# Two graph-attention layers on one core: norm transposes moved from TensorE to VectorE blocks and a pass through DRAM

## The chip, the cores and the metric

The kernel runs on one core of one Trainium2 chip. The metric is the device time of one execution in microseconds, lower is better. The kernel before takes 2702.04 us, the median of three runs between 2700.38 and 2702.28. The engines are called PE (TensorE; PEld is its weight load), DVE (VectorE), ACT (ScalarE), POOL (GpSimd) and SP (SyncE, which here issues the DMAs).

## The reference

64 graphs of 256 nodes with 512 features pass through two layers, each with a norm without weights and a relu in front and a residual around it. All numbers are 32-bit floats.

```
h = relu(layernorm(x))                       # 64 x 256 x 512
hW = h @ W                                   # 512 -> 256
alpha = softmax(leaky_relu(hW a0 + (hW a1)^T) masked by adj)
x = x + concat(alpha @ hW, hW)
h = relu(layernorm(x))
q, k, v = h @ Wq.T + bq, h @ Wk.T + bk, h @ Wv.T + bv     # 8 heads of 64
x = x + concat(softmax(q k^T / 8 masked by adj) v) @ Wo.T + bo
```

Both norms feed matrix products that contract over the features. The normed rows have nodes on the partitions, and the products want features there, so every normed tile has to be transposed.

## The kernel before

**Groups and steps.** Two graphs make a group: 512 rows, as four tiles of 128 rows by 512 features (index `t` or `r`, 0 to 3). There are 32 groups, software-pipelined in `bounded`. While the main loop does the attention of group g, the generator `project(g+1)` makes q, k and v of the next group (21 pieces, named u in the order below), `outputs` multiplies a finished graph by Wo and adds it to x (7 pieces, o), and `first_layer(g+2)` (pieces named s) does the first norm, the whole first layer and the second norm of the group after that. One turn of the loop is a period of four steps. A step begins with `weigh` (products pr and total, then on DVE the reciprocal r and the product oT) and `scores` (products sc, on ACT the exponentials p, on DVE two multiplications of p by the mask, on POOL the sums ps). After that it runs the pieces in an order written out by hand:

```
steps = ("uosuoosuosoosuos", "uusususususu", "uosoosuosoosuos", "uusususususu")
```

I count the steps 0 to 3 and the s pieces of a period s1 to s20, five to a step.

**Products in seven.** `project` and `outputs` use seven products of half-size blocks in the place of eight. For that POOL makes sums of the operands (`operand_sums`, L374 to L379: tile sums for the projections, o_sums for the outputs), and results are added up in PSUM banks or by DVE. In `outputs` the piece o3 accumulates into the bank that o1's DVE addition (`add`, L626 to L628) must have read, o5 needs o3's, o6 needs o4's, o7 needs o5's. Five PSUM banks (tag turn) rotate among the short-lived products, three more are held.

**The norm.** `stats` (L338) takes mean and variance of a tile with two DVE instructions. `norm_T` (L343) makes the variances safe (ve, L347) and has POOL raise them to -1/2 (rstd, L349). Then for each tile `put` (L359) lets DVE make the normed tile xn (L354) one tile ahead, PE transposes it in four 128 by 128 blocks into one bank pt (through `transpose`, L116), and ACT takes the bank into hT with the relu (L365). In the first layer each hT tile is used at once by the products ph; in the second, four puts fill hT for `project`, after which POOL makes the sums and adds the output bias to x (L470, four instructions).

**What sets the order.** PE instructions keep the order of the program text (`in_order`, L107). On the other engines a list scheduler orders the instructions when the program is built: among those it takes for ready it prefers the earlier one of the text, so an instruction whose inputs are there early can go ahead of earlier text that still waits. `after` (L96) adds an order between two instructions without a semaphore; before the change only `weight_sums` uses it. Each engine then runs its queue strictly in that order. SP issues all DMAs: one load of 1 MB per group into tile x (L125) and one store of 512 KB per graph (L654).

**Start and end.** Group 0's first layer runs alone (`last_bias` and the weight sums of q are put in at its third GAP), then `project(0)` together with group 1's first layer, then the loop. `judge` (L224) computes bounds on the inputs; its pieces are put in where a norm has a gap, over many periods, and its 56 products use blocks of Wq and Wk that it loads again. At the end a branch on its result either stops or runs a general version, which doesn't run here.

Of the kernel before, what the change touches and what calls it, by code (L numbers as in the profile page):

```python
# [23 lines left out]
LARGEST_VALUE = 1e6  # L24

# [17 lines left out]
def bounded(  # L43
# [23 lines left out]
    nc = tc.nc  # L67
    B, N, D = x.shape
# [17 lines left out]
    psum = ctx.enter_context(tc.tile_pool(name="psum", bufs=1, space=bass.MemoryType.PSUM))  # L86

# [15 lines left out]


# [13 lines left out]
    xg = x.rearrange("(g b) (t p) d -> g p (b t) d", b=GB, p=P)  # L118
    og = out.rearrange("(g b) (t p) d -> g p (b t) d", b=GB, p=P)
# [3 lines left out]
    def load(g):  # L123
        xs[g] = big.tile([P, GT, D], F32, tag="x", name=f"x{g}", bufs=4)
        nc.sync.dma_start(xs[g], xg[g])  # L125

    load(0)


# [14 lines left out]
    for c in range(HP):  # L144
        for s in range(2):
            nc.vector.scalar_tensor_tensor(
                prod, w0_sb[:, c, 2:], 1.0, a_b[:, s, :], op0=ALU.mult, op1=ALU.mult,
                accum_out=w0_sb[:, c, s : s + 1],
            )
    edge = att.tile([P, NT, N], F32, tag="e", name="edge")  # L150
    nc.vector.tensor_scalar(edge, adj_i, 0.0, None, op0=ALU.not_equal)
# [6 lines left out]
    nc.vector.tensor_copy(maskT, pt)  # L158

    nc.vector.reduce_max(bad[:, 0, :], edge, axis=AX.X)  # L160
    nc.vector.tensor_scalar(bad[:, 0, :], bad[:, 0, :], 0.0, None, op0=ALU.is_equal)
    nc.vector.tensor_tensor(edge, edge, adj_i, op=ALU.not_equal)
    nc.vector.reduce_max(bad[:, 1, :], edge, axis=AX.X)

    load(1)
    load(2)
# [29 lines left out]
    rexp = const.tile([P, GT], F32, name="rexp")  # L196
    nc.gpsimd.memset(rexp, -0.5)
    ones = const.tile([P, P], F32, name="ones")
    nc.gpsimd.memset(ones, 1.0)

    def weight_sums(name):
        w = w_sb[name]
        first = nc.vector.tensor_sub(w[:, :, T3, :], w[:, :, W22, :], w[:, :, W12, :])
        after(first, latest[0])
        nc.vector.tensor_sub(w[:, :, T1, :], w[:, :, W12, :], w[:, :, W11, :])
        nc.vector.tensor_sub(w[:, :, T2, :], w[:, :, W22, :], w[:, :, T1, :])
        nc.vector.tensor_sub(w[:, :, T4, :], w[:, :, W21, :], w[:, :, T2, :])

    def last_bias():


        pb = mm("pb")
        for q in range(NQ):
            for half in range(2):
                b = small.tile([P, P], F32, tag="power", name=f"bv_{q}_{half}", bufs=1)
                nc.vector.tensor_scalar(b, ones, bv_col[:, half, q : q + 1], None, op0=ALU.mult)
                matmul(
                    pb, b, w_sb["o"][:, half, 2 * q : 2 * q + 2, :],
                    start=(q == 0 and half == 0), stop=(q == NQ - 1 and half == 1),
                )  # L220
        nc.vector.tensor_add(b_out, pb, b_out)


    def judge():  # L224
# [5 lines left out]
        nc.vector.memset(part, 0.0)  # L230
        junk = att.tile([P, D], F32, tag="junk", name="junk", bufs=1)

        def squares(col, *srcs):
            sums = small.tile([P, HP], F32, tag="sums", name=f"sums{col}", bufs=2)
            for i, src in enumerate(srcs):
                nc.scalar.activation(
                    junk[:, : src.free_size()], src, AF.Square, accum_out=sums[:, i : i + 1]
                )
            nc.vector.reduce_sum(part[:, col : col + 1], sums[:, : len(srcs)], axis=AX.X)

        for s in range(2):
            squares(s, w0_sb[:, :, s])
        squares(2, *[w0_sb[:, c, 2:] for c in range(HP)])
        wv = att.tile([P, HP, D // HP], F32, tag="block", name="wv_block", bufs=1)
        sums = small.tile([P, HP], F32, tag="sums", name="sums3", bufs=2)
        for c in range(HP):
            nc.sync.dma_start(
                wv, wvT[:, c * P : (c + 1) * P].rearrange("(c p) o -> p c o", p=P)
            )
            nc.scalar.activation(  # L250
                junk, wv.rearrange("p c o -> p (c o)"), AF.Square, accum_out=sums[:, c : c + 1]
            )
        nc.vector.reduce_sum(part[:, 3:4], sums, axis=AX.X)
        squares(4, bcol["q"])
        squares(5, bcol["k"])
        squares(6, bv_col.rearrange("p h q -> p (h q)"))
        nc.vector.reduce_max(part[:, 7:8], bad.rearrange("p a t -> p (a t)"), axis=AX.X)
        yield
        heads = const.tile([P, P], F32, name="heads")
        nc.vector.memset(heads, 0.0)  # L260
        for j in range(2):
            nc.vector.memset(heads[j * DH : (j + 1) * DH, j * DH : (j + 1) * DH], 1.0)
        rowsq = const.tile([P, 2, HP], F32, name="rowsq")
        for n, (name, src) in enumerate((("q", wqT), ("k", wkT))):
            for hp in range(HP):
                w = att.tile([P, HP, P], F32, tag="block", name=f"w{name}_block{hp}", bufs=1)
                nc.sync.dma_start(
                    w, src[:, hp * P : (hp + 1) * P].rearrange("(c p) o -> p c o", p=P)
                )
                yield  # L270
                gram = mm(f"gram_{name}{hp}")[:, :P]
                for c in range(HP):
                    matmul(
                        gram, w[:, c, :], w[:, c, :], start=(c == 0), stop=(c == HP - 1)
                    )
                a = small.tile([P, P], F32, tag="power", name=f"power_{name}{hp}_0", bufs=1)
                nc.vector.tensor_mul(a, gram, heads)
                yield
                for i in range(3):
                    square = mm(f"square_{name}{hp}_{i}")[:, :P]  # L280
                    matmul(square, a, a, start=True, stop=True)
                    if i < 2:
                        a = small.tile(
                            [P, P], F32, tag="power", name=f"power_{name}{hp}_{i + 1}", bufs=1
                        )
                        nc.vector.tensor_copy(a, square)
                    else:
                        nc.scalar.activation(
                            junk[:, :P], square, AF.Square, accum_out=rowsq[:, n, hp : hp + 1]
                        )  # L290
                    yield
        nc.vector.reduce_sum(part[:, 8:10], rowsq, axis=AX.X)
# [3 lines left out]
        nc.vector.tensor_scalar(norm, total, 1e-30, None, op0=ALU.add)  # L296
        power = const.tile([P, 10], F32, name="power")
        nc.gpsimd.memset(power, 0.5)
        nc.gpsimd.memset(power[:, 7:8], 1.0)
        nc.gpsimd.memset(power[:, 8:10], 1.0 / 32)  # L300
        nc.gpsimd.tensor_tensor(norm, norm, power, op=ALU.pow)
# [5 lines left out]
        nc.vector.tensor_add(test[:, 0:1], norm[:, 0:1], norm[:, 1:2])  # L307
        nc.vector.tensor_scalar(
            test[:, 0:1], test[:, 0:1], root / LARGEST_SCORE, None, op0=ALU.mult
        )  # L310
        nc.vector.tensor_scalar(side, norm[:, 8:10], root, None, op0=ALU.mult)
# [31 lines left out]
    def norm_T(src, mv, name):  # L343
# [15 lines left out]
        def put(t, dst):  # L359
            if t + 1 < GT:  # L360
                normed(t + 1)
# [34 lines left out]
    def first_layer(g):  # L396
# [11 lines left out]
        for t in range(GT + 1):  # L408
# [4 lines left out]
            if t == 0:  # L413
                continue
# [659 lines left out]
```

## Time and profile before

| | before |
|---|---|
| median of the timed runs | 2702.04 us |
| the profiled execution, its own time | 2699.08 us |
| span of the profile | 2697.3 us |
| mean granted TensorE clock | 0.993 |
| PE busy | 2620.4 us |
| DVE busy, instructions | 1669.7 us, 2558 |
| POOL busy | 1230.0 us |
| ACT busy | 835.9 us |
| DMA traffic, mean | 29 GB/s |
| xn, 128x512, DVE (L354) | 256 instructions, 893 ns mean, 523 to 1559 ns |
| statistics of a tile, DVE (L340) | 256 instructions, 680 ns mean |
| hT from pt, ACT (L365) | 256 instructions, 599 ns mean |

The profile is of one execution. Its span runs from the first to the last instruction; 1.8 us lie around it. In a row of the groups, the parts are line, engine, operation, output and inputs with their shapes and the count, then the busy time, the mean of one, and how long the engine stood idle before these instructions and what ended that. In the chain of waits each row is a start, a duration and what ran; it leads back from the last instruction to what released each one. In the windows view each stretch has busy time and number of instructions of PE, PEld, DVE, ACT and POOL, then the granted clock, the DMA share and GB/s. Busy PE time counts overlapping matmuls once, but the end of a matmul is modelled.

### The profile page before, as it was taken

The page shows a single profiled execution, that of the slowest core. Times are in us where ns is not written, and L with a number is a line of the kernel's source. Part 1 is how long each engine was busy: PE and PEld are TensorE (multiplying, and loading weights), DVE is VectorE, ACT ScalarE, POOL GpSimd, SP SyncE. Part 2 cuts the span into 40 slices and gives each one's busy share as a digit, 9 for nine tenths or more (in the row PEclk, how much of TensorE's full clock was granted, in tenths as well). Part 3 has the DMA queues.
Part 4 walks back from the last instruction along what each step waited for, and adds up shares of the span by engine and source line. Part 5 has one row for each costly group of instructions (what it writes and reads, how often), then busy time and mean ns, then how long its engine had stood idle before and what let it go on. Part 6 is the DMA issues. An engine that isn't in the chain of part 4 may idle for free.

```text
span 2697.3 us, 41512 instructions
## 1 busy us (share of the span) xinstructions
PE 2620.4 (97%) x17150; PEld 2118.8 (79%) x17150; DVE 1669.7 (62%) x2558; ACT 835.9 (31%) x1771; POOL 1230.0 (46%) x1004
## 2 busy tenths in 40 slices
PE   5999999999999999999999999999999999999997
PEld 3888888878888887887788888788878878878874
DVE  5666566666557665566665576665576656666544
ACT  2333232333332333323333323333333333233321
POOL 2353355443445443545434454435455335445343
PEclk8999999999999999999999999999999999999998
DMA  5000101000001010000000000000000000000000
GB/s 164 1 12 32 36 24 36 13 32 32 28 32 36 9 36 32 24 32 9 32 32 24 32 32 9 32 32 24 32 32 9 32 32 24 32 17 23 17 16 25
DMA packets 45890, 78.49 MB, mean 29 GB/s; under 512 B 3712, under 2 KB 10624, under 8 KB 45696
## 3 DMA queue, kind: packets, MB, share of 16 engines
q1 hardware_dynamic: 45696, 75.77, 8.1%
q8 instruction: 137, 2.24, 0.3%
q14 instruction: 57, 0.47, 0.1%
HBM read 42.21 MB, written 33.55 MB: 28 GB/s over the span
## 4 chain that ended last, share of the span: by engine, by line
PE 89%; DVE 8%; POOL 1%; issue 1%; DMA 0%; ACT 0%; DVEq 0%
PE pq L113 15%; PE pv L113 14%; PE py L113 13%; PE pk L113 13%; PE pr L113 9%; PE ph L113 8%; PE sc L113 7%; PE po L113 4%; PE pt L116 4%; DVE p L573 3%; DVE r L604 2%; PE total L113 2%; DVE k L544 1%; DVE oT L605 1%; PE pn L116 1%
## 5 line engine op out<-in xcount | busy, mean ns | idle before, releaser
L573 DVE TENSOR_TENSOR p<-p,maskT 128x1024 f32<-128x1024 f32 x256 | 398.6, 1588 | 0.6 <-ACT p L572 0.5
L572 ACT ACTIVATE p<-sc 128x512 f32<-128x512 f32 x512 | 264.4, 602 | 380.9 <-PE sc L113 380.9
L574 POOL TENSOR_TENSOR ps<-p 128x512 f32<-128x512 f32 x256 | 366.2, 1447 | 0.0
L628 DVE TENSOR_TENSOR x<-py,x 128x256 f32<-128x256 f32 x448 | 187.6, 419 | 272.8 <-PE py L113 266.9
L604 DVE RECIPROCAL r<-total 128x256 f32<-128x256 f32 x128 | 224.5, 1754 | 194.6 <-PE total L113 194.6
L113 PE MATMUL py<-wo_sb,o_sums 128*128 128x256 f32 x1024 | 266.5, 384 | 26.4 <-DVE x L628 21.6
L420 POOL TENSOR_TENSOR x<-H,x 128x256 f32<-128x256 f32 x128 | 87.7, 685 | 443.0 <-ACT H L419 441.9
L113 PE MATMUL pr<-p,v 128*32 128x256 f32 x4096 | 251.8, 385 | 5.8 <-DVE p L573 5.8
L113 PE MATMUL sc<-q,k 64*128 64x256 f32 x2048 | 255.7, 389 | 0.0
L113 PE MATMUL pq<-sums,wq_sb 128*128 128x256 f32 x1024 | 246.7, 384 | 4.2 <-POOL sums L377 3.7
L113 PE MATMUL ph<-w_sb,hT 128*128 128x258 f32 x1024 | 246.1, 383 | 0.0
L113 PE MATMUL pk<-sums,wk_sb 128*128 128x256 f32 x1024 | 244.8, 382 | 0.0
L113 PE MATMUL pv<-wv_sb,sums 128*128 128x256 f32 x1024 | 242.0, 379 | 0.1
L113 PEld LDWEIGHTS sc<-q,k 64*128 64x128 f32 x2048 | 187.2, 186 | 69.7 <-issue 52.6
L113 PEld LDWEIGHTS py<-wo_sb,o_sums 128*128 128x128 f32 x1024 | 191.2, 192 | 62.9 <-POOL o_sums L377 37.6
L365 ACT ACTIVATE hT<-pt 128x512 f32<-128x512 f32 x256 | 153.1, 599 | 266.0 <-PE pt L116 265.7
L354 DVE TENSOR_SCALAR xn<-x,mv,rstd 128x512 f32<-128x512 f32 x256 | 225.8, 893 | 9.5 <-PE pt L116 4.9
L376 POOL TENSOR_TENSOR o_sums<-oT 128x256 f32<-128x256 f32 x64 | 106.2, 1660 | 262.6 <-DVE oT L605 262.6
L113 PEld LDWEIGHTS pq<-sums,wq_sb 128*128 128x128 f32 x1024 | 190.1, 191 | 39.1 <-issue 9.9
L113 PEld LDWEIGHTS ph<-w_sb,hT 128*128 128x128 f32 x1024 | 195.7, 192 | 28.6
L113 PEld LDWEIGHTS pk<-sums,wk_sb 128*128 128x128 f32 x1024 | 189.3, 190 | 33.9 <-issue 9.9
L113 PEld LDWEIGHTS pr<-p,v 128*32 128x32 f32 x4096 | 121.1, 110 | 112.2 <-issue 39.7
(145 smaller groups left out, 4054.4 us busy)
## 6 DMA issues: line engine op xcount, KB each, us to landing
x<-in_x_dram SPq DMA_DIRECT2D x32, 1024.0 KB, 5.5
out_dram<-x SPq DMA_DIRECT2D x64, 512.0 KB, 2.8
wq_sb<-in_L_gnn_Wq_dram SPq DMA_DIRECT2D x2, 512.0 KB, 11.7
wk_sb<-in_L_gnn_Wk_dram SPq DMA_DIRECT2D x2, 512.0 KB, 12.4
wv_sb<-in_L_gnn_Wv_dram SPq DMA_DIRECT2D x2, 512.0 KB, 11.4
wo_sb<-in_L_gnn_Wo_dram SPq DMA_DIRECT2D x8, 128.0 KB, 3.3
wv_block<-in_L_gnn_Wv_dram SPq DMA_DIRECT2D x4, 256.0 KB, 3.0
wq_block<-in_L_gnn_Wq_dram SPq DMA_DIRECT2D x4, 256.0 KB, 2.9
```

The source lines that it names most:

```text
L113: in_order(nc.tensor.matmul(*args, **kwargs))
L116: in_order(nc.tensor.transpose(*args))
L354: latest[0] = nc.vector.tensor_scalar(xn[t], src[:, t, :], mv[:, t, 0:1], rstd[:, t : t + 1], op0=ALU.subtract, op1=ALU.mult,).ins.name
L365: nc.scalar.activation(dst, pt, AF.Relu)
L376: nc.gpsimd.tensor_add(sums[:, 0], a21, a22)
L420: nc.gpsimd.tensor_add(xt[:, t, F1:], H[:, t, 2 : F1 + 2], xt[:, t, F1:])
L544: nc.vector.tensor_add(part(1, 1), first, p7)
L572: nc.scalar.activation(pair[:, j], sc[j], AF.Exp, scale=scale)
L573: nc.vector.tensor_mul(pair, pair, maskT[:, None, :, :].to_broadcast([P, 2, NT, N]))
L574: nc.gpsimd.tensor_add(ps[:, 2 * i : 2 * i + 2, :], pair[:, :, 0, :], pair[:, :, 1, :])
L604: nc.vector.reciprocal(r, total)
L628: nc.vector.tensor_add(to, out, to)
```

## The change

From group 1 on, the four transposes of a tile leave PE. `turn` (two tiles, one graph, at a time) has DVE transpose each xn inside 32 by 32 blocks (one instruction for a tile), SP stores the result to a scratch tensor in DRAM (passed, 512 KB), and four more DMAs of 128 KB read it back with the blocks moved to their place (moved). ACT applies the relu from moved, in SBUF, into hT. Group 0 still uses PE. Each GAP between `turn` and `put` is a piece s at which the generator issues nothing more.

A wrapper remembers the latest instruction of each engine in the order of the text, and `not_sooner` puts an instruction behind it: statistics, xn and the DVE transposes on DVE, the relu on ACT, the first of the operand sums on POOL. The bias additions to x leave `first_layer` and are issued in step 1. `judge` runs at the start, takes its blocks from the weights in SBUF, and does four products per bank. x is loaded by graph, in seven buffers of 512 KB; hT0 becomes one buffer for a graph; the three kept buffers become two of one tag. `last_bias` uses POOL for its four columns, each in its own place. The order string of the steps is the same.

```diff
+    def not_sooner(engine, operation, *args, **kwargs):
+        last = engine.last
+        after(getattr(engine, operation)(*args, **kwargs), last)
...
-    def load(g):
-        xs[g] = big.tile([P, GT, D], F32, tag="x", name=f"x{g}", bufs=4)
-        nc.sync.dma_start(xs[g], xg[g])
+    def load(g, b):
+        xs[g, b] = big.tile([P, NT, D], F32, tag="x", name=f"x{g}_{b}", bufs=7)
+        nc.sync.dma_start(xs[g, b], xg[g, b])
...
+        if vector.last:
+            not_sooner(vector, "bn_stats", st, src[t])
...
+        def norm(b):
+            tiles = slice(b * NT, (b + 1) * NT)
+            ve = small.tile([P, NT], F32, tag="ve", name=f"ve{name}_{b}")
+            vector.tensor_scalar(ve, mv[:, tiles, 1], EPS, None, op0=ALU.add)
+            rstd = small.tile([P, NT], F32, tag="rstd", name=f"rstd{name}_{b}")
+            gpsimd.tensor_tensor(rstd, ve, rexp, op=ALU.pow)
+            for t in range(NT):
+                r = b * NT + t
+                xn[r] = att.tile([P, D], F32, tag="xn", name=f"xn{name}_{r}", bufs=2)
+                not_sooner(
+                    vector, "tensor_scalar", xn[r], src[r], mv[:, r, 0:1], rstd[:, t : t + 1],
+                    op0=ALU.subtract, op1=ALU.mult,
+                )
+        def turn(b):
...
+            J = P // S
+            xt = att.tile([P, J, HP, NT, S], F32, tag="xt", name=f"xt{name}_{b}")
+            moved = att.tile([P, J, HP, NT, S], F32, tag="moved", name=f"moved{name}_{b}")
+            passed = dram.tile([P, J, HP * NT * S], F32, tag="passed", name=f"passed{name}_{b}")
+            for t in tiles:
+                not_sooner(
+                    vector, "transpose",
+                    xt[:, :, :, t % NT, :], xn[t].rearrange("p (c j a) -> p j c a", j=J, a=S),
+                )
+                turned[t] = moved[:, :, :, t % NT, :].rearrange("p i c n -> p c i n")
+            nc.sync.dma_start(passed, xt.rearrange("p j c t n -> p j (c t n)"))
+            for j in range(J):
+                nc.sync.dma_start(
+                    moved[j * S : (j + 1) * S].rearrange("a i c t n -> a i (c t n)"),
+                    passed.rearrange("(i a) j e -> j a i e", a=S)[j],
+                )
+        def put(b, dst):
+            for t in range(NT):
...
+                    not_sooner(scalar, "activation", to, turned[b * NT + t], AF.Relu)
...
     def operand_sums(quads, sums):
         a11, a12, a21, a22 = quads
-        nc.gpsimd.tensor_add(sums[:, 0], a21, a22)
+        not_sooner(gpsimd, "tensor_add", sums[:, 0], a21, a22)
...
     def first_layer(g):
...
+        norm(0)
         yield GAP
...
+        turn(0)
+        norm(1)
+        yield GAP
+        turn(1)
+        yield GAP
+        yield GAP
+        put(0, hT[0])
+        yield GAP
+        for r in range(GT):
...
+            if r == NT - 1:
+                put(1, hT[1])
             yield
...
             stats(mv, xt, r, f"1_{g}")
+            if r == 2:
+                norm(0)
+            elif r == 3:
+                turn(0)
+            yield
...
+        norm(1)
         yield GAP
+        turn(1)
+        yield GAP
+        put(0, hT[:, :, :N])
+        yield GAP
+        put(1, hT[:, :, N:])
...
-        for t in range(GT):
-            nc.gpsimd.tensor_add(xt[:, t, :], xt[:, t, :], b_out)
-        yield
+        yield
+
+    def residual(g):
+        for b in range(GB):
+            for t in range(NT):
+                xt = xs[g, b][:, t, :]
+                gpsimd.tensor_add(xt, xt, b_out)
...
+    verdict = judge()
+    for piece, _ in enumerate(first_layer(0)):
+        if piece == 9:
+            next(verdict)
+        if piece == 14:
             last_bias()
+            next(verdict)
+        if piece == 16:
             weight_sums("q")
+    residual(0)
...
-            if step == 1 and g + 3 < NG:
-                load(g + 3)
+            if step == 1 and g + 1 < NG:
+                residual(g + 1)
+            if step % 2 and g + 3 < NG:
+                load(g + 3, b)
```

With it the s pieces of a period hold: s1 the four statistics and `norm(0)` of the first layer; s2 `turn(0)` and `norm(1)`; s3 `turn(1)`; s4 nothing; s5 `put(0)`; s6 to s9 ph, with `put(1)` at s7; s10 pn and e; s11 nothing; s12 to s15 po with its statistics, `norm(0)` of the second layer at s14 and `turn(0)` at s15; s16 `norm(1)`; s17 `turn(1)`; s18 `put(0)`; s19 `put(1)` and the operand sums.

## The prediction

> **What bounds the kernel now.** I read the page first: shares, then the chain that ended last.
>
> ```profile
> PE 2620.4 (97%) x17150; PEld 2118.8 (79%) x17150; DVE 1669.7 (62%) x2558; ACT 835.9 (31%) x1771; POOL 1230.0 (46%) x1004
> ...
> PE 89%; DVE 8%; POOL 1%; issue 1%; DMA 0%; ACT 0%; DVEq 0%
> ```
>
> PE holds nearly all of the span; no other engine has two thirds of it. A share hides the stages, so the windows view comes next, for the four steps of one late period (rows in order: step 0, 1, 2, 3).
>
> ```profile
> 1994.66:2015.14 20.48, 20.48 (x141) 16.82 (x144) 10.86 (x14) 6.74 (x14) 12.10 (x10) 1.00 0.00 1
> 2015.14:2037.76 22.62, 22.62 (x149) 18.54 (x152) 7.69 (x9) 8.08 (x19) 7.09 (x6) 1.00 0.19 70
> 2037.76:2058.12 20.36, 19.35 (x129) 15.41 (x132) 15.92 (x29) 4.96 (x11) 6.56 (x5) 1.00 0.00 1
> 2058.12:2076.42 18.30, 18.30 (x133) 14.70 (x136) 17.21 (x27) 6.02 (x11) 12.68 (x10) 1.00 0.08 30
> ```
>
> The period is 81.76 us. PE is idle for 1.0 us of it, in step 2, and the granted clock is full. DVE (the third busy time) is unequal: 17.2 us of 18.3 in step 3, 10.9 of 20.5 in step 0. Whatever leaves PE shortens the period, until DVE is late for it.
>
> The chain in order of time gives PE's pitch, and DVE's timeline its queue, from the start of a step 0 at 2076.42.
>
> ```profile
> 2076.42 1.86 PE pr L113 x32
> ...
> 2086.89 0.44 PE pt L116 x4
> 2087.32 1.73 PE pq L113 x8
> ```
>
> ```profile
> 2078.78 1.76 DVE L604 RECIPROCAL r<-total 128x256 f32<-128x256 f32 x1 [3.16 <-PE total L113]
> 2080.58 0.69 DVE L605 TENSOR_TENSOR oT<-pr,r 128x512 f32<-128x512 f32 x1
> 2081.18 3.23 DVE L573 TENSOR_TENSOR p<-p,maskT 128x1024 f32<-128x1024 f32 x2
> 2084.34 0.41 DVE L628 TENSOR_TENSOR x<-py,x 128x256 f32<-128x256 f32 x1
> ```
>
> A tile's four transposes hold PE for 0.44 us (the 156.2 us of busy time are 152 ns for each, with overlap; the pitch is 109 ns). DVE starts r when total ends and reaches o1's addition 7.92 us into the step.
>
> **Removed from PE.** 31 groups by 8 tiles by 0.435 us: **-107.9 us** (busy time would say -151; the chain decides). That none of it is saved is the other end.
>
> **judge.** Its 112 instructions at 0.108 us (the chain has 0.22 for two of its squares; 12.1 us) leave later steps for the first 100 us. There PE is busy 48.4 of the first 80 us, so up to all 12 can hide: **-6**, between -12 and 0. Its loads vanish from an idle queue: nothing.
>
> **Start.** The chain has 5.74 us of bias additions on POOL (53.57 to 59.31) ahead of the sums that the third product waits for; they now come after. The four rounds of last_bias (45.40 to 52.80) no longer alternate with DVE. Against that, group 1 turns on DVE beside `project(0)`, whose pieces are 1.73 us apart, so s2 to s6 is some 8 us and the round trip below is 8 to 9. **-6**, between -15 and +5. Sum so far: 2697.3 - 107.9 - 6 - 6 = **2577.4**, if nothing else is late.
>
> **Added to DVE.** 248 transposes of 128x512. The trace has none. Nearest rows:
>
> ```profile
> L354 DVE TENSOR_SCALAR xn<-x,mv,rstd 128x512 f32<-128x512 f32 x256 | 225.8, 893 | 9.5 <-PE pt L116 4.9 <-POOL rstd L349 3.6 <-issue 0.2
> L604 DVE RECIPROCAL r<-total 128x256 f32<-128x256 f32 x128 | 224.5, 1754 | 194.6 <-PE total L113 194.6
> L340 DVE BATCH_NORM_STATS2 st<-x 128x6 f32<-128x512 f32 x256 | 169.1, 680 | 15.8 <-DMA x<-in_x_dram 4.9
> ```
>
> I take 0.69 (L340's 0.68; additions of 128x512 take 0.69): 171 us, DVE 1841 in all. Ends: 0.52 (the fastest xn) and 1.75 (the reciprocal); no less than nothing, since it is an instruction more.
>
> The Trainium skill speaks against this edit. "VectorE: DVE Perf Modes", section "The three transpose paths", gives 311 ns for 128x128 bf16 on VectorE, within 32 by 32 blocks only, and its "Rules for kernel authors" give a 128x128 transpose to TensorE when PSUM will do. By that rule the tile's 0.44 us stay on PE and the time stays at 2697; by the busy shares it pays to move them. An estimate from the page's figure is four times 311 ns, 1.24 us a tile, 0.55 above my value.
>
> **Moved on DVE.** Statistics, xn and transposes no longer fill DVE's holes, but stand behind earlier text. Step 3 is relieved; step 0, 17.4 us of PE without its three pts (1.3) and its ph (1.74), now holds DVE work of 9.1 (10.86 less two xn) + 4 x 0.85 statistics + 4 x 0.9 xn + 4 x 0.69 + 0.3 = 19.2 us. By hand, in us from the step's start: o1's addition ends at 8.3; four statistics (0.75 apart) at 11.3; ve 11.4; while POOL makes rstd (its ps end at 11.9, 1.0 more), the additions of u2, o2, o3 end at 12.8; two xn at 14.7; two transposes at 16.0; ve; o4's addition at 16.5. PE, with its pieces at 1.73 (u) and 0.865 (o), has o5 done at 13.9 and then stands at o6, whose bank waits for o4's addition: **2.6 us**. Should rstd be later, o4's addition goes first and the stall is nothing, but the norm is later by as much. Today such waits are small:
>
> ```profile
> PE py L113 <- DVE x L628: 21.6, 27, 1.0
> ```
>
> Step 1 takes over the ph (23.9 us; DVE about 10 and the spill) and step 3 has slack. In step 2 DVE gets 15.9 + 1.8 + 1.3 less the hoisted 1.3, some 17.7 of 20.4 us: the 1.0 stays. Loop turns 0 to 29 do this: 30 x 2.6 = **+78**, between 0 (DVE's holes suffice) and 200 (below).
>
> **The round trip.** SP waits for both transposes, stores 512 KB and waits for that to land before it issues four loads of 128 KB.
>
> ```profile
> out_dram<-x SPq DMA_DIRECT2D x64, 512.0 KB, 2.8
> wq_block<-in_L_gnn_Wq_dram SPq DMA_DIRECT2D x4, 256.0 KB, 2.9
> ```
>
> With 0.37 us per issue: 0.4 + 2.8 + 4 x 0.4 + 2.9 = 7.7 us (5.9 if the loads land at once, 9 if each of them is like wo_sb's 3.3 under load). Behind the waits SP queues the out store and the x loads; x is read a period later, so nobody waits. Some 130 MB more over 2650 us are 49 GB/s on top of 29; the load phase reaches 400.
>
> First layer: transposes at 16.0, moved at 23.7, relu 25; ph is due at 17.4 + 2.6 + 7.7 = 27.7. Hidden. Second layer: `turn(1)` in step 3 runs at about 14.5 (r to p end at 8.3 there, v's addition, rstd 1.0 to 2.4, two xn, transposes), moved at 22.1, which is 5.6 into the next step 0; relu 6.8; two sums (1.28 each) 9.4; u3 needs them at 10.5. Hidden by 1.1 us. Relu from SBUF: ACT's nearest row is 630 ns (wv_block) against 599 from PSUM, 8 us on an engine at 31%: nothing.
>
> "DMA: Bandwidth & Descriptors", section "Two DMAs through the same engine are not ordered", says that a transfer must wait for the first one's completion count; the trace agrees (load L125 after the store into its buffer waited 74.5 us in 28 times), and the 2.8 us can't be overlapped.
>
> **Bias additions to x.** Same four instructions of POOL in step 1 (7.1 of 22.6 us busy) in place of step 3 (12.7 of 18.3): nothing. Other edits (two kept buffers, one hT0, seven x buffers): their next use is two pieces or more away, nothing; a kept buffer that isn't free would cost a piece, 1.7 us.
>
> **Forecast.** 2577.4 + 78 = 2655.4 of span. The profiled execution lies 1.8 above its span, and the median 3.0 above that: **2660**.
>
> **Rivals.**
> - *Hidden altogether* (DVE in the holes, stall 0): 2577.4 + 4.7 = 2582. For it: DVE 62%, and a list scheduler fills rstd's wait. Against: 19.2 us into 17.4.
> - *The round trip takes the wait over* (slower). `put(1)` stands in ACT's queue ahead of step 0's exponentials. They are ready 3.45 us into the step (ACT's timeline), moved 5.6: with two relus they start 3.4 late, and masks, o1's addition and o3's product with them. Price 30 x (2.6 + 3.4) = 180: 2577.4 + 180 + 4.7 = **2762**. It decides from 4.0 us a period on (119.9 / 30), so from some 1.4 us of lateness. For it: such waits of ACT exist today:
>
> ```profile
> ACT hT L365 <- PE pt L116: 265.7, 156, 17.3
> ```
>
> Against: if the scheduler knows the latency, it puts the exponentials first.
> - *A transpose costs like the reciprocal*, 1.75: o4's addition 2.1 later and the second pair as much, 2.6 + 4.2 = 6.8 a period: 2577.4 + 30 x 6.8 + 4.7 = 2786.
> - *It doesn't do what it says*, the round trip being waited for at every relu of the first layer too (7.7 a half group): above 2800, or the transposes staying: 2690.
>
> **How the numbers follow.** Forecast 0.36 (stalls of 1.3 to 3.7: its own range 2620 to 2693), hidden 0.26, near no change (stalls near 4.0) 0.06, round trip 0.23, dear transposes 0.05, the last 0.04. A measurement of this kernel tells some 0.2% from no change (5 us). Faster: 0.36 + 0.26 = 0.62; same 0.06; slower 0.23 + 0.05 + 0.04 = 0.32. The range 2580 to 2750 leaves out the upper half of the round trip and the dear transposes.
>
> **What would show it.** Right: pt only 32 instructions; DVE transposes near 0.69; a period near 80.3 with step 0 near 20 and PE's largest wait "py <- DVE x", some 2.6 us a period; step 3 near 16.5; POOL's sums ending some 9 us into step 0. Wrong: PE without waits and a period of 78 (hidden); or ACT standing at hT for DMA, and then PE waiting for p, o_sums or kept (round trip); or a transpose above 1 us.

## The result and the profile after

The changed kernel takes **3034.62 us** (median of 4 runs, 3032.70 to 3035.32), the kernel before 2701.21 us (2699.42 to 2702.28): a ratio of **1.1234**, 95% interval 1.1214 to 1.1253. The forecast was 2660 us, in a range of 2580 to 2750. It is wrong in its sign and by 375 us.

The shares first, then the engines of the chain that ended last, from the page of the kernel after.

```profile
PE 2665.9 (88%) x16158; PEld 2112.8 (70%) x16158; DVE 1743.9 (58%) x2847; ACT 821.5 (27%) x1759; POOL 1200.1 (40%) x1072
...
PE 68%; POOL 16%; DVE 13%; issue 2%; ACT 1%; DMA 0%; SPq 0%; ACTq 0%; DVEq 0%; POOLq 0%
```

PE has 992 instructions fewer (248 tiles of four transposes), and yet more busy time than before, 2665.9 against 2620.4. POOL, with 1% of the chain before, holds 16% of it. POOL's busy share says nothing of it (it fell from 46% to 40%); the chain says who is waited for.

The windows view of one late period, in the order step 1, 2, 3, 0 (columns: the stretch, its length, the busy time of PE, PEld, DVE, ACT and POOL with the number of their rows, PE's granted clock, DMA share, GB/s).

```profile
1615.18:1639.10 23.92, 23.92 (x152) 19.67 (x156) 8.10 (x9) 9.45 (x23) 7.71 (x7) 1.00 0.34 96
1639.10:1663.30 24.20, 21.08 (x129) 16.60 (x132) 16.07 (x32) 4.95 (x11) 8.54 (x8) 0.93 0.00 1
1663.30:1680.38 17.08, 16.77 (x116) 13.13 (x120) 13.87 (x18) 4.87 (x9) 9.09 (x8) 1.00 0.51 172
1680.38:1707.33 26.95, 20.48 (x120) 15.90 (x124) 15.81 (x29) 6.07 (x13) 11.90 (x11) 0.81 0.12 42
```

The period is 92.15 us, 10.39 longer than before: step 1 +1.30, step 2 +3.84, step 3 -1.22, step 0 +6.47. Thirty times that is 312 of the 333 us; another 16 lie ahead of the loop (the first pr starts at 143.31 instead of 126.97). Step 1 is what the forecast had (23.9), and step 3 is 0.6 us over its 16.5. The loss sits in the two steps that hold `outputs`, and in both the clock column falls below 1.00.

Who makes PE wait, from the waits view of PE (us in total, times, longest):

```profile
PE py L135 <- POOL o_sums L35: 301.1, 63, 6.5
```

Twice a period PE stands at o3, the first product that needs an operand sum of the outputs. Before, PE waited 4.2 us in all for o_sums, and its largest wait was 21.6. POOL's timeline in step 0, which starts at 1680.38, shows why the sum is late.

```profile
1686.44 1.26 POOL L35 TENSOR_TENSOR ps<-p 128x512 f32<-128x512 f32 x1 [9.93 <-DVE p L35]
1687.66 3.47 POOL L35 TENSOR_TENSOR sums<-hT 128x512 f32<-128x512 f32 x2
1691.10 1.26 POOL L35 TENSOR_TENSOR sums<-sums,hT 128x512 f32<-128x512 f32 x1
1692.43 1.27 POOL L35 TENSOR_TENSOR sums<-hT,sums 128x512 f32<-128x512 f32 x1
1693.66 1.26 POOL L35 TENSOR_TENSOR ps<-p 128x512 f32<-128x512 f32 x1
1694.88 0.72 POOL L35 TENSOR_TENSOR o_sums<-oT 128x256 f32<-128x256 f32 x1
1695.67 0.72 POOL L35 TENSOR_TENSOR o_sums<-o_sums,oT 128x256 f32<-128x256 f32 x1
```

The operand sums come last. In the text `scores`, which holds ps, stands ahead of `outputs`, and `not_sooner` on the first operand sum puts it behind whatever POOL's instruction was last in the text: both ps, which wait for the exponentials and for DVE's masks. Before, the scheduler had taken the three o_sums ahead of the ps, 5.3 to 9.4 us into the step. POOL's rows in the kernel before, in a step 0 that starts at 1994.66:

```profile
1999.92 1.71 POOL L376 TENSOR_TENSOR o_sums<-oT 128x256 f32<-128x256 f32 x1
2001.70 1.59 POOL L377 TENSOR_TENSOR o_sums<-o_sums,oT 128x256 f32<-128x256 f32 x1
2003.37 0.73 POOL L379 TENSOR_TENSOR o_sums<-oT,o_sums 128x256 f32<-128x256 f32 x1
2004.06 2.50 POOL L574 TENSOR_TENSOR ps<-p 128x512 f32<-128x512 f32 x2
```

Now oT, which the o_sums need, is there at 1685.2 and they start at 1694.88, behind both ps and the four projection sums. PE's rows around the gap:

```profile
1688.95 1.03 PE L135 MATMUL py<-wo_sb,oT 128*128 128x256 f32 x4
1696.45 2.07 PE L135 MATMUL py<-wo_sb,o_sums 128*128 128x256 f32 x4 [6.47 <-POOL o_sums L35]
1698.32 3.62 PE L135 MATMUL pq<-sums,wq_sb 128*128 128x256 f32 x8
```

Behind the gap a piece of project takes 3.4 us up to the next row instead of 1.73, and a piece of outputs 1.9 instead of 0.865: the granted clock is 0.81 over this step. In step 2 the same happens at a smaller scale: both ps end at 1648.5, o_sums at 1650.0, PE waits 3.12 us, clock 0.93. Against their usual pitch the rows behind the two gaps are stretched by 2.9 and 1.8 us.

### The profile page after: what moved, and what is told of

Same layout as the page of the kernel before. It is cut to its first block, busy times and chain, and to the rows that moved or that the text cites. A ratio compares the mean times of both kernels' runs of the same rounds, so it can differ in the third digit from the quotient of the medians.

```text
span 3032.3 us, 40906 instructions
## 1 busy us (share of the span) xinstructions
PE 2665.9 (88%) x16158; PEld 2112.8 (70%) x16158; DVE 1743.9 (58%) x2847; ACT 821.5 (27%) x1759; POOL 1200.1 (40%) x1072
## 4 chain that ended last, share of the span: by engine, by line
PE 68%; POOL 16%; DVE 13%; issue 2%; ACT 1%; DMA 0%; SPq 0%; ACTq 0%; DVEq 0%; POOLq 0%
PE pk L135 11%; PE py L135 11%; PE pq L135 11%; PE pv L135 9%; PE pr L135 7%; PE ph L135 7%; POOL ps L35 6%; POOL sums L35 6%; PE po L135 4%; DVE r L35 4%; DVE p L35 4%; PE sc L135 3%; POOL o_sums L35 3%; PE total L135 2%; DVE oT L35 1%
## 5 line engine op out<-in xcount | busy, mean ns | idle before, releaser
L35 POOL TENSOR_TENSOR ps<-p 128x512 f32<-128x512 f32 x256 | 396.9, 1561 | 600.9 <-DVE p L35 600.9
L135 PE MATMUL py<-wo_sb,o_sums 128*128 128x256 f32 x1024 | 307.1, 434 | 301.1 <-POOL o_sums L35 301.1
L35 DVE TENSOR_TENSOR p<-p,maskT 128x1024 f32<-128x1024 f32 x256 | 374.4, 1485 | 21.7 <-ACT p L35 21.6
L135 PE MATMUL pq<-sums,wq_sb 128*128 128x256 f32 x1024 | 299.6, 445 | 9.3 <-POOL sums L35 8.8
L35 POOL TENSOR_TENSOR o_sums<-oT 128x256 f32<-128x256 f32 x128 | 145.8, 1139 | 385.2 <-DVE oT L35 383.5
L35 POOL TENSOR_TENSOR rstd<-ve,rexp 128x2 f32<-128x2 f32 x128 | 90.8, 710 | 501.1 <-DVE ve L35 484.6
L135 PEld LDWEIGHTS pq<-sums,wq_sb 128*128 128x128 f32 x1024 | 228.7, 226 | 61.5 <-ACT p L35 9.9
L35 DVE TENSOR_SCALAR xn<-x,mv,rstd 128x512 f32<-128x512 f32 x256 | 178.1, 708 | 162.5 <-POOL rstd L35 162.4
L35 DVE TENSOR_TENSOR k<-pk,kept_k 128x512 f32<-128x512 f32 x96 | 66.1, 688 | 317.2 <-PE pk L135 317.0
L35 ACT ACTIVATE kept_q<-pq,bq_sb 128x256 f32<-128x256 f32 x192 | 81.1, 479 | 564.4 <-PE pq L135 564.4
L135 PEld LDWEIGHTS pv<-wv_sb,sums 128*128 128x128 f32 x1024 | 194.5, 190 | 28.5 <-DVE v L35 2.1
## 6 DMA issues: line engine op xcount, KB each, us to landing
wq_sb<-in_L_gnn_Wq_dram SPq DMA_DIRECT2D x2, 512.0 KB, 10.9
```

The lines of the kernel that those rows point to most:

```text
L35: instruction = getattr(self.engine, operation)(*args, **kwargs)
L135: in_order(nc.tensor.matmul(*args, **kwargs))
```

## The experiments

Theory *order*: most of the loss is the order of the operand sums on POOL. Rival *trip*: it is the passes through DRAM, which make hT and the projection's sums late. Rival *VectorE*: transposes and their orders make DVE late, as the forecast's own term of 78 us has it. A fourth share, *rest*, is judge, the moved bias additions and the buffers.

**The operand sums freed**: one line of the changed kernel.

```diff
-        not_sooner(gpsimd, "tensor_add", sums[:, 0], a21, a22)
+        gpsimd.tensor_add(sums[:, 0], a21, a22)
```

> The changed kernel with one line put back: the first of the operand sums on POOL is no longer ordered behind the last POOL instruction of the text. Theory order (o_sums stand behind both ps, which wait for the masks; PE waits for them at o3 in steps 0 and 2): the wait py <- o_sums (301 us) all but goes, the period falls from 92.15 to about 83.6 us, the time to about 2780; what stays is a wait of pq <- sums of some 4 us at u3, because the second norm arrives late from DRAM. Theory round trip (the late arrival alone fills POOL's place for the o_sums): the sums still come ahead of o_sums, the wait moves little, time above 2950. Theory of the forecast (DVE is late for o4's addition): no change, since DVE's order is the same.

Measured: 2831.53 us, ratio 1.0487 (1.0469 to 1.0504), period 85.76: 203 us and 6.4 us a period under the changed kernel. PE's waits now:

```profile
PE pq L135 <- POOL sums L35: 119.6, 32, 6.9
PE py L135 <- DVE x L35: 47.0, 88, 1.8
...
PE py L135 <- POOL o_sums L35: 4.2, 2, 2.1
```

The wait at o_sums is gone, and another takes its place once a period: in step 0, u3 waits 3.67 us for the projection's sums. Of the 47.0 us at x, 27.1 lie in step 2, where the kernel before has its 21.6; the other 19.9 lie in step 0, at o6 and behind it. There the wait is 1.81 us (with 0.46 and 0.16 behind it) in only two of 30 periods, whose clock column reads 1.00; in the others the clock is lower behind the gap at u3 (0.93 or 0.86), PE comes later to o6, and less of this wait or none is left. Step 0 lasts 24.5 us either way. So order is the largest share and not the whole.

**The order alone, put on the kernel before**: the first operand sum goes behind the last ps, whose name `pool_last` holds; nothing else.

```diff
-        nc.gpsimd.tensor_add(sums[:, 0], a21, a22)
+        first = nc.gpsimd.tensor_add(sums[:, 0], a21, a22)
+        if pool_last[0]:
+            after(first, pool_last[0])
```

> The kernel before with one order added: the first operand sum behind the last ps of the text. All transposes stay on PE. Theory order: PE gets the wait py <- o_sums in steps 0 and 2, 1 to 3 us in each and something on top for a lower granted clock, so 100 to 180 us more, 2800 to 2880. Theory round trip or DVE: within 10 us of 2702.

Measured: 2877.41 us, ratio 1.0655 (1.0637 to 1.0673). PE's wait for o_sums is 151.2 us in 63 times (mostly 1.75 us in a step 0, 3.12 in a step 2). The period isn't steady: it lies between 85.9 and 90.9 us (median 87.6), with a step 2 of 22.5, 24.2 or 25.4 us; the last section shows why. One dependency that computes nothing costs 178 us in a kernel without any pass through DRAM. By an estimate some 125 of them are waits (151.2 less the 4.2 for o_sums and the 21.6 for x that they replace) and some 53 the clock (0.975 granted over the span of 2880.1 us, against 0.993 of 2697.3). With the trip beside it the same order costs 203, because the late projection sums stand between ps and o_sums in POOL's queue (the rows above).

**All tiles turned by PE**, all orders kept.

```diff
-        by_pe = g == 0
+        by_pe = True
```

> The changed kernel with every transpose on PE (group 0's way for all groups): no DVE transposes, no pass through DRAM, all the orders and moves kept. Theory order: still far above before, 2800 to 2880, with py <- o_sums as the first wait of PE. Theory round trip: near 2700 or below, since judge and the start alone save some 12 us. Theory DVE: between, since the transposes' 5.4 us a period leave DVE.

Measured: 2997.68 us, ratio 1.1102 (1.1083 to 1.1120), period 91.3 (median). A miss for all theories: no tile passes through DRAM and the time is still 11% over. The wait for o_sums is 159.0 us in 63 times as in the run above, and PE now waits for xn (38.6 us in 31 times, of which 26.7 in step 0, 0.92 a time), because the ordered xn come late and the transposes stand in PE's own order. Another 22.2 us are a wait of sc for ACT's exponentials, which the run with all tiles on PE and everything free takes up. Where the orders stay, moving the transposes back buys 37 us.

**Second norm on PE, operand sums freed**: the first norm still passes through DRAM.

```diff
-        norm, turn, put = norm_T(xt, mv, f"1_{g}", by_pe)
+        norm, turn, put = norm_T(xt, mv, f"1_{g}", True)
```

> The changed kernel with the operand sums free, and the second norm transposed by PE (the first by DVE and DRAM). The sums of the projections can start as early as before. Theory order plus late arrival: no large wait is left, the period is 81.8 less four transposes of a tile (1.7 us), near 80, time 2620 to 2650. If the DRAM pass of the first norm or DVE's longer queue costs PE, ph <- hT or py <- x shows it and the time is above 2680.

Measured: 2727.20 us, ratio 1.0100 (1.0083 to 1.0117), period 82.38, first pr at 127.56. 104 us under the run with both norms through DRAM: the second norm's pass is a loss, though it takes 124 tiles off PE. The first norm's isn't seen as a wait for DRAM. What is left is the forecast's own stall, "py <- DVE x", 81.6 us in 114 times: 52.9 in step 0, where the forecast has it, and 26.3 in step 2, where the kernel before has it too. My expectation was 77 us or more too low: it left out that stall and the rest's 40 us, measured further on.

**All of the norms' instructions free, both norms through DRAM.** From here on, "free" also takes `not_sooner` off the statistics, xn, the VectorE transposes and the relus.

```diff
-                not_sooner(
-                    vector, "tensor_scalar", xn[r], src[r], mv[:, r, 0:1], rstd[:, t : t + 1],
-                    op0=ALU.subtract, op1=ALU.mult,
-                )
+                vector.tensor_scalar(
+                    xn[r], src[r], mv[:, r, 0:1], rstd[:, t : t + 1],
+                    op0=ALU.subtract, op1=ALU.mult,
+                )
```

> The run with the operand sums freed, and also the orders taken off the statistics, xn, the VectorE transposes and the relus; both norms still pass through DRAM. What then fills VectorE's holes is up to the scheduler. Theory (two separate costs: the orders on VectorE make its additions to x late, some 1.8 us of PE per period; the second norm's round trip ends late, 3.7 us): the first goes, the second stays: period 85.8 - 1.8 = 84.0 us, 2831 - 55 = some 2777 us, PE's largest wait pq on POOL's sums. Rival (the forecast's rival 'hidden altogether': once the scheduler may fill holes, everything is hidden): period near 78.3 and a time of 2590 to 2620. Rival 2 (these orders are not what makes VectorE late; it has too much to do): no change, 2820 to 2840.

Measured: 2908.18 us, ratio 1.0772 (1.0754 to 1.0790), period 88.75. All three expectations missed: it is 77 us slower than with the orders. The scheduler draws the next group's first norm into step 3, where the second norm already is. DVE's queue there, ahead of v's addition that PE waits for (start, us, row):

```profile
1616.84 1.25 DVE L35 BATCH_NORM_STATS2 st<-x 128x6 f32<-128x512 f32 x2
1618.01 0.30 DVE L35 BATCH_NORM_AGGREGATE mv<-st 128x2 f32<-128x6 f32 x2
1618.34 0.17 DVE L35 TENSOR_SCALAR ve<-mv 128x2 f32<-128x2 f32 x1
1619.33 1.00 DVE L35 TENSOR_SCALAR xn<-x,mv,rstd 128x512 f32<-128x512 f32 x2 [0.82 <-POOL rstd L35]
1620.24 0.68 DVE L35 TENSOR_TENSOR v<-pv,kept_v 128x512 f32<-128x512 f32 x1
```

PE waits 4.90 us for that v ("PE pv <- DVE v", 144.3 us in all), and that pv then takes 3.78 us instead of 1.9. So the orders on the first norm do what an order is for; they are not mere loss.

**The same, with the second norm on PE** (the run above and the edit of the run before it).

> First norm by VectorE and DRAM, second norm turned by PE, operand sums and all of the norms' instructions free for the scheduler. Theory (the stalls py on x of some 2.0 us a period come from the orders on VectorE): period 82.4 - 2.0 = 80.4, 2727 - 60 = 2667 us, so faster than the kernel before by over 1%. Rival (VectorE is late because of the work, not of its order): 2715 to 2735.

Measured: **2675.48 us, ratio 0.9909 (0.9893 to 0.9926)**: 0.9% faster than the kernel before, period 80.98. With one norm on DVE there is room for drawing it forward: the stalls at x fall from 81.6 to 26.3 us, all of these in step 2, and step 0 lasts 17.37 us instead of 20.01. A smaller wait comes instead, pv for v in step 3 (27.7 us, 29 times).

**The second norm a piece sooner, everything free, both through DRAM**: the empty piece behind pn and e is left out.

```diff
         yield
-        yield GAP
         mv = small.tile([P, GT, 2], F32, tag="mv", name=f"mv1_{g}")
```

> As the run with everything free and both norms through DRAM, but the second norm starts one piece of the first layer sooner: the empty piece behind the second layer's scores is left out, so statistics, xn, the transposes and the trip through DRAM begin some 5 us sooner. Theory (the second norm costs only because its operands land some 5 us after the end of their step): the wait of pq on POOL's sums goes, period 84.0 - 3.7 = 80.3, 2777 - 110 = some 2667 us. Rival (POOL's queue holds the sums behind its other work, whatever the landing): pq still waits 2 us or more a period, 2730 to 2780.

Measured: 2801.95 us, ratio 1.0377 (1.0359 to 1.0394), period 85.24. The named wait is gone (pq on POOL's sums: once, 6.3 us) and step 0 takes 18.1 us, so at that end the theory held; but step 3 takes 23.9, its pv waiting for kept_v and v (74.4 and 39.9 us) as in the run with everything free. The time is out by 135 us.

**Group 1's first norm on PE too**, so that nothing passes through DRAM ahead of the loop (the second norm is on PE in this run anyway): an edit of the fastest run.

```diff
-        by_pe = g == 0
+        by_pe = g < 2
```

> As the run with the second norm on PE and everything free, but the first norm of group 1, too, is turned by PE, so that nothing passes through DRAM before the loop. It costs PE 8 x 0.435 = 3.5 us. Theory (the start is longer because group 1's trip through DRAM lies open there): first pr some 5 to 10 us sooner, the time 2 to 7 us under that run. Rival (the trip is hidden at the start): 3 to 4 us over it.

Measured: 2677.71 us, ratio 0.9916 (0.9900 to 0.9933), first pr at 132.07 instead of 129.0: the rival held, with the loop starting 3.1 us later and the time 2.2 us over. The first norm's trip is hidden at the start; the late start of the changed kernel is the second norm's (first pr at 141.93 with it through DRAM, 127.56 without).

**The operand sums freed, all other orders kept, second norm a piece sooner.**

> The run with only the operand sums freed (both norms through DRAM, all other orders kept), and the second norm one piece of the first layer sooner. Theory (pq waits 3.7 us a period on POOL's sums because the second norm's operands land late): that wait goes, 2831 - 110 = some 2720 us. Rival (VectorE and POOL are in the way whatever the landing): above 2800.

Measured: 2822.02 us, ratio 1.0457 (1.0440 to 1.0475), period 85.45. My theory fell, and its 5 us with it: step 3 is shorter too, so the last load lands 0.8 us into step 0 (median) instead of 2.4, and ACT runs the relus from 4.5 to 5.6 us into the step in both runs, behind the first pair of exponentials. pq still waits 2.46 us a period. POOL's timeline of step 0, from 1659.87:

```profile
1664.87 1.64 POOL L35 TENSOR_TENSOR o_sums<-oT 128x256 f32<-128x256 f32 x1 [10.74 <-DVE oT L35]
1666.59 1.74 POOL L35 TENSOR_TENSOR o_sums<-o_sums,oT 128x256 f32<-128x256 f32 x1
1668.41 0.73 POOL L35 TENSOR_TENSOR o_sums<-oT,o_sums 128x256 f32<-128x256 f32 x1
1669.09 2.49 POOL L35 TENSOR_TENSOR sums<-hT 128x512 f32<-128x512 f32 x2
1671.54 1.26 POOL L35 TENSOR_TENSOR sums<-sums,hT 128x512 f32<-128x512 f32 x1
```

The sums that u3 needs stand behind the three o_sums, which wait for oT; POOL is idle for 10.74 us before. So here it isn't the trip's length that costs, it is the place of the relus on ACT and of the sums on POOL: three of them and three o_sums don't fit between oT (5 us into the step) and u3 (some 10).

**Everything free but the first norm's first statistics, second norm a piece sooner**, both through DRAM. The new argument of `stats` says whether the order is kept.

```diff
         for t in range(GT):
-            stats(mv, xt, t, f"0_{g}")
+            stats(mv, xt, t, f"0_{g}", t == 0 and g > 0)
```

> Both norms through DRAM, operand sums free, second norm one piece sooner; of the orders only the one on the first norm's first statistics is kept, so that the first norm isn't drawn into the step before. Theory (what cost in the two runs with everything free was the first norm drawn into step 3, where v's additions then waited behind it; what cost in the first run was the late second norm): both waits go, period 80 to 81.5 with some stall at x left, 2660 to 2710 us. Rival (VectorE with both norms is simply late somewhere: the stall moves to py behind x, over 3 us a period): 2740 to 2790.

Measured: 2721.98 us, ratio 1.0083 (1.0066 to 1.0099), period 82.20. Both named waits go: pq waits for POOL's sums twice in the whole run (8.1 us), pv never. The last load lands 0.5 us ahead of step 0 (median), the relus run from 0.6 us into it, ahead of the exponentials, and POOL has the sums from 1.8. The step starts at 1599.71.

```profile
1601.52 2.49 POOL L35 TENSOR_TENSOR sums<-hT 128x512 f32<-128x512 f32 x2 [6.71 <-ACT hT L35]
1603.98 1.27 POOL L35 TENSOR_TENSOR sums<-sums,hT 128x512 f32<-128x512 f32 x1
1605.21 1.71 POOL L35 TENSOR_TENSOR o_sums<-oT 128x256 f32<-128x256 f32 x1
```

That run is 100 us under the one before it, with the same pass of the same tiles through DRAM, and 46 over the fastest run, so in this arrangement the second norm's pass loses some 46 us and not 104. It lies 12 us above the range given for it, as 71.6 us at x (83 times) and 25.5 us of total behind x are left: first norm's xn waits for rstd, which is last in POOL's queue, and the additions to x stand behind xn. PE is busy 78.4 us of the period.

**Everything free, all tiles on PE.** What remains is *rest*. The edit of the fastest run:

```diff
-        by_pe = g == 0
+        by_pe = True
```

> Everything of the change but the passes through DRAM and the orders: both norms turned by PE, operand sums and the norms' instructions free. What is left are the judge at the start, the moved bias additions, the buffers. Theory (these parts are near nothing, as the forecast has it): 2685 to 2705. Rival (they have a price of their own, in the start or in the period): above 2710. Against the run with the first norm through DRAM (2675) it gives what those 124 tiles off PE are worth: 54 us at 0.435 each if all of it is saved.

Measured: 2739.60 us, ratio 1.0150 (1.0133 to 1.0167), period 83.00, first pr at 131.92. The rival held: the rest costs 40 us, 5 ahead of the loop and 1.2 a period. The place is in step 1, from PE's timeline:

```profile
1628.21 1.14 PE L135 MATMUL sc<-q,k 64*128 64x256 f32 x8
1630.09 1.61 PE L135 MATMUL sc<-q,k 64*128 64x256 f32 x8 [0.74 <-ACT p L35]
1631.63 1.99 PE L135 MATMUL pq<-sums,wq_sb 128*128 128x256 f32 x8
```

From sc to pq it takes 3.42 us; in step 0 of the same run 1.93. The second pair of scores waits for a bank that the exponentials empty. The kernel before has no such wait: it spreads the tiles over the steps, while here four tiles are turned in step 0, and two of them hold their banks until the relus of step 1, which leaves three of five for four banks of scores. That this is the reason is read from the code and not tried by itself; with the first norm off PE the wait is gone.

**First norm on PE, second through DRAM and a piece sooner, everything free.**

```diff
-        by_pe = g == 0
+        by_pe = True
...
-        norm, turn, put = norm_T(xt, mv, f"1_{g}", by_pe)
+        norm, turn, put = norm_T(xt, mv, f"1_{g}", False)
```

> First norm on PE, second norm by VectorE and DRAM and one piece sooner, everything free. Theory (the second norm, too, can leave PE when it is early enough and VectorE has room): 54 us under the run with all on PE, some 2640 to 2660. Rival (the scheduler draws the first norm's statistics and xn into step 3 and v's additions wait behind rstd, as with both norms): 2700 to 2800.

Measured: 2811.16 us, ratio 1.0419 (1.0402 to 1.0437), period 85.55. The rival held, and the time is 11 us beyond its upper end: pv waits for kept_v (56.7 us in 29 times); in the period looked at, ACT's kept_v waits 4.14 us for v's addition, which stands on DVE behind xn, and xn waits for rstd. Against all on PE it is 72 us slower. So the pass through DRAM pays for the first norm alone, and for the second in none of the arrangements tried.

## Why the prediction was wrong, point by point

The runs form a ladder from before to after, one share at a time (medians, against the kernel before of the same batch):

| step | us | forecast for it |
|---|---|---|
| rest: all on PE, all free, against before | +40 | -12 |
| first norm off PE by DVE and DRAM | -64 | -54 |
| orders on the norms' instructions (second norm on PE) | +52 | +78, both norms |
| second norm off PE by DVE and DRAM | +104 | -54 |
| order on the operand sums | +203 | no term |
| all | +335 | -42 |

(The forecast's -107.9 is split by tiles, 124 and 124. Measured less forecast, the rows give +52, -10, -26, +158 and +203, together 377 of the 375 us. The ladder ends 2 us from 333, as the batches ran on different chips. A share depends on the rung it is taken at: the last one is 178 on the kernel before.)

- **The step that failed** is the sum itself: it has no term for the order on the operand sums. The diff lists that edit, the section on the change names it, and none of the prediction's parts prices it. Its timeline of step 0 has "POOL makes rstd (its ps end at 11.9, 1.0 more)", which is the queue of before, with the o_sums ahead of both ps; in the changed kernel the ps end 7.3 and 14.5 us into the step and the second o_sums 16.0. The price could be had from the trace of before. In its step 0 the second mask ends 8.1 us in; one ps more (1.25) and two o_sums (0.8 each) make 10.9, and o3 is due at 9.5: 1.4 us late. In its step 2 the same sum is 7.9 + 1.25 + 1.6 = 10.7, and o3 is due at 7.8: 2.9. The order alone measured 1.75 and 3.12. In the changed kernel it is 203 us, 54% of the error.
- **"moved 5.6 into the next step 0; relu 6.8; two sums (1.28 each) 9.4; u3 needs them at 10.5. Hidden by 1.1 us."** The trip itself was sized well: the store landed 2.8 us after its issue, as taken, and the loads 3.3 after theirs (2.9 taken), with the four issues taking 1.73 together; the last load landed 2.2 us into step 0 (median), 3.4 sooner than forecast, mostly because `turn(1)` ended 12.1 us into step 3 and not 14.5. (The 74.5 us that the prediction quotes are loads that waited for a store out of their buffer, not into it; that the loads of the pass wait for its store shows in SP's rows of the changed kernel: store issued at 1675.38, first load at 1678.09.) The end failed, in the queues behind the landing. The relus ran only 4.4 to 5.6 us into the step, behind the first pair of exponentials on ACT. Product 6 reads the second sum, which is the third that POOL computes, not the second; and the forecast put the sums into a free POOL, while ps or o_sums stood ahead of them. With the operand sums freed the third sum ends 14.2 us into step 0 instead of 9.4, and PE waits 3.67. In the run with the second norm sooner and the other orders kept the sums still stand behind o_sums; in the run in which it is also free they don't; there the relus, too, go ahead of the exponentials, and the time falls by 100 us with the same trips. Why the list scheduler puts the relus there in one run and not in the other stays open. So the place in the queues, more than the trip, sets the price: +104 instead of -54, and +46 in the best arrangement tried.
- **The rest, "-6" and "-6"**: measured +40. judge's work was rightly seen to leave later steps, but the start grew by 5 us and the period by 1.2. No part of the prediction had that; the wait for banks in step 1 explains the period's part if the reading of the code is right, which no run tries by itself.
- **-107.9** held as PE's own work. The four steps without their tiles, each taken from a run where it holds no wait, last 17.37 (step 0, fastest run) + 23.93 + 19.33 + 16.51 (steps 1, 2 and 3, second norm sooner, orders kept) = 77.1 us; before, PE is busy 80.75, less 8 x 0.435 makes 77.3. What didn't hold is that the work taken off PE comes off the time: the first norm's half gave 64 us (54 for the tiles; the wait at sc of 22.2 us went with them and one of 27.7 at v came), the second's half nothing.
- **DVE's transposes, 0.69**: 0.68 us on average over 248. The estimate from the Trainium skill, "VectorE: DVE Perf Modes", section "The three transpose paths", was 1.24 us; the measurement decides, it is about half. The same page's "Rules for kernel authors" give a 128x128 transpose to TensorE when PSUM will do: the first norm speaks against it here (64 us gained by moving it, or 24 against the kernel before, which doesn't pay for the bank wait), the second for it (104 us lost), by the order in other engines' queues.
- **DVE's stall at o6, 2.6 us a period, +78**: the mechanism is there in step 0 at the place that was named, hidden in the changed kernel behind the longer wait at o3 (DVE catches up while PE stands) and, with the operand sums freed, mostly behind the one at u3. It stands free in the run with the second norm on PE and the orders kept: step 0 lasts 20.01 us there against 17.37 with the orders off, 2.64 longer. So this term was right in kind and size, though nothing of it is seen in the changed kernel's time.
- **Rival "hidden altogether"** fell with the forecast. **Rival "the round trip takes the wait over"** had the right side and the wrong engine: it put the queue on ACT, where `put(1)` would hold up the exponentials. The trace has the first pair of exponentials ahead of the relus, as the rival's own "against" had it, the relus at 4.4 us, and next to no wait of ACT for the loads (5.9 us in 10 times in the whole run); the queue that decided was POOL's.
- **The clock** had no term. The rows behind the two long gaps are stretched by 4.7 us together, of the 10.4 that the period grew by.

## What to carry to other kernels

Price every line of a diff, above all those that only set an order: take the engine's timeline in the profile of before, put the instruction at its new place by hand, and follow each consumer to the end; here one such dependency costs 178 us by itself. An engine that is busy 40% of the time can be the bound when its queue has a fixed order, so work that is moved off the critical engine must be checked against the places in the other engines' queues that its product passes (here POOL's), not against their shares. And an order can be worth keeping on one instruction of a chain and ruinous on another: of the variants tried, the two that beat the kernel before drop all orders and move the first norm only.

## What the runs showed of the hardware

- What a gap of PE costs in clock depends on where it lies on a fixed grid of 3.41 us, and not on its length alone. In the kernel before with the order added, step 2 has a gap of 2.2 to 3.3 us in every period, and of 31 such steps the clock column reads 1.00 in 11, 0.93 or 0.92 in 10 and 0.87 in 10. Here are two of them, each with a gap of 3.12 us, and below each the two stretches of the grid in which its gap lies (columns as above):

```profile
1639.51:1662.01 22.50, 19.38 (x126) 15.42 (x125) 15.37 (x29) 5.02 (x11) 5.52 (x5) 1.00 0.00 1
1645.46:1648.87 3.41, 1.99 (x10) 1.41 (x8) 2.59 (x5) 0.00 (x0) 3.23 (x2) 1.00 0.00 0
1648.87:1652.28 3.41, 1.71 (x8) 1.53 (x9) 0.42 (x1) 0.00 (x0) 2.29 (x4) 1.00 0.00 0
1812.91:1838.26 25.35, 22.23 (x126) 17.43 (x125) 15.37 (x29) 5.02 (x11) 5.52 (x5) 0.87 0.00 1
1819.53:1822.94 3.41, 1.32 (x7) 0.81 (x5) 1.92 (x4) 0.00 (x0) 3.41 (x3) 1.00 0.00 0
1822.94:1826.35 3.41, 2.38 (x6) 1.93 (x7) 0.27 (x1) 0.00 (x0) 1.62 (x3) 0.50 0.00 0
```

  The first gap is shared out between two stretches, and PE is busy for half of each or more; the second leaves PE busy for 1.32 us of one stretch, and the next two, of which one is shown, are granted half the clock. In all the traces of this case the clock is full or half, and it changes only on such a grid: 308 full-clock stretches in which PE was busy for less than 40% were all followed by a half-clock one, none of the 10339 above 53% was, and of the 206 between, 109 were. So a mean of 0.93 over a step of 24.2 us is one such stretch at half clock.
- DVE and POOL can slow one another when both are busy. In the run with both norms through DRAM and everything free, a mask multiplication of 128x1024 takes 1.22 us ahead of POOL's ps and 2.29 beside ps and an addition to x, which itself takes 2.26 instead of 1.27. In the run with only the operand sums freed and the second norm sooner, two o_sums take 1.64 and 1.74 us beside DVE's mask multiplications and the third 0.73 behind them (rows above), while those multiplications keep 1.22 and 1.23. Which of the two is slowed isn't settled here. A sum of durations from rows that stand alone is too short where both engines are busy.
